# Moving part of a feed-forward stage from beside a convolution to beside a projection, with longer pieces of delta in memory

## The chip, the cores and the metric

The kernel runs on one core of a Trainium2 chip. A core has five engines that each work through an instruction queue of their own, in a fixed order: PE (TensorE, matrix products), DVE (VectorE), ACT (ScalarE), POOL (GpSimd) and SP (SyncE, which here issues every DMA). Sixteen DMA engines move data between HBM, the large memory, and SBUF, the memory on the chip. PE writes its products to PSUM, eight banks of 128 x 512 floats. The metric is the time of one execution in microseconds (us) on the device.

## The reference

The input is eight images of 96 channels and 64 x 64 positions. Layer 0 is a state-space block in four directions, layer 1 a linear attention and a feed-forward net on fp8:

```python
x = x + L0(group_norm(x))
  # L0, per image:
  xi, z = split(layernorm(x) @ in_proj_w.T + in_proj_b)          # 192 + 192 channels
  xi    = silu(depthwise_conv3x3(xi) + conv_b)
  xs    = [rows, columns, rows reversed, columns reversed]        # 4 directions, L = 4096 positions
  dts, B, C = split(x_proj_w[k] @ xs[k])                          # 6 + 16 + 16
  delta = softplus(dt_proj_w[k] @ dts + dt_proj_b[k])             # 192 channels
  h[t]  = exp(delta[t] * A) * h[t-1] + (delta[t] * u[t]) * B[t]   # 16 states a channel
  y[t]  = sum over states (h[t] * C[t]) + D * u[t]
  out   = out_proj(layernorm(sum over directions y) * silu(z))
t = tokens(x)
t = t + attention(layernorm(t))        # without softmax: q (k^T v)
t = t + ffn(layernorm(t))              # x, W1, W2 rounded to fp8 (5,2), sums to fp16, relu
```

## The kernel before

The eight images are worked on in four pairs; two images fill 384 rows, 192 channels each, in three tiles T of 128 partitions (the third holds 64 rows of each image). The positions are cut into eight chunks of F = 512. The loop from L883 runs five times, and in each pass lays the end of the pair before (`old`) beside the beginning of the next (`new`):

1. `back` of the old pair (L682: sums of the four directions, output projection, keys and values) together with `project` of the new one (L238: group norm, layer norm, input projection), L916.
2. `tail` of the old pair (L819) together with `convolve` of the new one (L311), L932.
3. `gates` (L349): 24 Silu activations on the convolution's result.
4. `prepare` (L365): for two orders of positions, eight chunks and two directions each, 32 steps in all. A step makes B, C and dts with three products (`pt`), copies them to `S`, makes delta with one product for each T (`pq`) and a Softplus, multiplies it by u (`du`), cuts delta into three bf16 parts (`dp`, on ACT, DVE and POOL by turns) and writes all of it to scratch in HBM (`bs`, `cs`, `du`, `dl`).
5. `scan` (L435): 128 steps (four directions, 32 chunks of TC = 128 positions), the recurrence itself, eight scan instructions a step on DVE, their factors made by PE and ACT (L570, L577), the driving term by POOL (L552).

The first pass has no old pair and the last no new one, so the last pass is `back` and `tail` alone.

`tail` works on 16 pieces (two images, eight chunks), each in three stages: attention's product `pa` and the sum `t`, and the layer norm (L668: product `ncp`, square, product `nvp`, Ln and Exp, product with `ncp` to the fp8 tile `tq`); the first fp8 product `pf` with relu; the second one and the sum `ot`, which is stored. A step of `tail` starts one piece and carries the two before it one stage further, so that 18 steps do the whole. `convolve` yields 19 times: two of the three tiles are summed on DVE, nine taps in two halves (L342, L344), the third on PE as nine products with diagonal matrices (L328). `together` (L870) alternates between two such generators, `m` steps of the second spread over `n` of the first, and then runs both to their ends.

The order in which the code emits is a priority. Outside `scan` a planner puts the instructions of each engine in order before the run, by that priority and by when it reckons their inputs and buffers to be there; on the chip each engine keeps that order. Three things bind it. Activations that need a table (Ln and Exp, Silu, Softplus) keep the order of the program among each other (`table`, L177; the tables of Ln and Exp are loaded at L180, the others by the activation's own line). Pools limit what is in flight: `tps` gives `tail` six PSUM banks, `p1cp` gives `convolve` two; `prepare` has three for `pt` and four for `pq`; SBUF tiles of both have two or three buffers. And all DMAs stand in one queue, on SP. `scan` orders by hand: in step s, `load(s + 1)` brings the next chunk's delta (`dm`, two buffers), `fetch` the driving term (`dut`), `load_bc` and `diagonal` B and C.

`dl`, delta in scratch, has the shape [4 directions, 32 chunks, 3 parts, 16, 24 rows, 128 positions] in bf16, so one row of one chunk is 256 bytes in a piece. The weights `winT`, `xw` and `dtw` are loaded and laid out once, ahead of the loop, and stay in SBUF.

## Time and profile before

| | us |
|---|---|
| median of 3 runs | 11845.06 |
| lowest, highest | 11842.54, 11851.63 |
| the profiled execution, its span | 11820.4, 11818.4 |
| first pair: scans begin | 639 |
| second pair: scans of the first end; convolution and tail from; gates from; first Softplus; last writes of delta; scans begin | 2535; 2980; 3162; 3183; 3508; 3534 |
| last pass: tail alone from | 11633 |

Over the whole span PE is busy 73%, DVE 74%, ACT 58%, POOL 68%, and the DMA queue's packets take 75.4% of the sixteen engines' time. A profile covers one execution. Its page has the busy time of each engine in 40 slices; a table by stage gives the same for chosen stretches, with the clock that the throttle granted to PE (1.00 is full speed). In rows of groups and of time, an entry like `L344 DVE SCALAR_TENSOR_TENSOR xi<-y,c_convw,xi` names the line, the engine, the operation and its output and inputs; what stands in brackets is how long the engine was idle before, and what it waited for. In rows of waits come the line that waited, what it waited for, the sum in us, how often and the longest.

### The profile page before, as it was taken

The numbers are of one execution on the slowest core, as the hardware profiler recorded it, in microseconds if no ns is written. First come the engines' busy times: TensorE is split into PE (matmuls) and PEld (weight loads), VectorE is DVE, ScalarE is ACT, GpSimd is POOL, SyncE is SP. The second block draws the span as 40 slices with busy tenths as digits, with TensorE's granted clock in tenths as the row PEclk, the third lists the DMA queues.
The fourth block names the chain that finished last, engine by engine and source line by source line (L and its number), as shares of the span: only waits on it lengthen the run. The fifth ranks groups of instructions, "written<-read, shape, count | busy, mean of one in ns | idle before, by whom it ended". The sixth has DMA issues, their size and how long they took to land. (4 is left out here: it accounts for less than half of the span.)

```text
span 11818.4 us, 387513 instructions
## 1 busy us (share of the span) xinstructions
PE 8675.0 (73%) x170112; PEld 5662.7 (48%) x170112; DVE 8756.4 (74%) x6465; ACT 6900.1 (58%) x12176; POOL 7986.7 (68%) x2770
## 2 busy tenths in 40 slices
PE   7856666779877666667986666667898666667787
PEld 2245555544225555554422555555442355555542
DVE  5489999963549999995355999999454699999922
ACT  3556666644456666664455666666445566666623
POOL 0489999960249999994025999999313699999910
PEclk8678888879768888888976888888896788888896
DMA  2988888875398888886459888888646988888862
GB/s 79 215 198 201 198 203 201 198 160 134 97 215 195 203 201 200 204 195 149 120 125 209 197 202 199 197 199 199 148 99 156 203 199 199 200 198 200 193 132 63
DMA packets 1655919, 2092.92 MB, mean 177 GB/s; under 512 B 962179, under 2 KB 1307348, under 8 KB 1651412
## 3 DMA queue, kind: packets, MB, share of 16 engines
q1 hardware_dynamic: 1654228, 2068.13, 75.4%
q8 instruction: 1335, 21.87, 0.9%
q14 instruction: 356, 2.92, 0.1%
HBM read 1604.17 MB, written 463.54 MB: 175 GB/s over the span
## 5 line engine op out<-in xcount | busy, mean ns | idle before, releaser
L588 DVE TENSOR_TENSOR_SCAN h<-da,dbu 128x774 f32<-128x774 f32 x4096 | 7028.4, 1760 | 646.5 <-ACT da L577 443.1
L552 POOL TENSOR_TENSOR dbu<-dut,bc 128x1536 f32<-128x1536 f32 x2048 | 7083.1, 3506 | 578.1 <-ACT dbu L549 478.7
L577 ACT ACTIVATE da<-da 128x768 f32<-128x768 f32 x4092 | 3254.2, 797 | 2155.9 <-PE da L570 2117.6
L606 PE MATMUL yp<-h,cw 128*32 128x48 f32 x131072 | 3145.2, 246 | 1126.0 <-issue 1110.7
L570 PE MATMUL da<-dm,aw 128*128 128x128 bf16 x24576 | 2502.0, 251 | 1447.2 <-DVE h L588 1098.1
L606 PEld LDWEIGHTS yp<-h,cw 128*32 128x32 f32 x131072 | 2548.9, 155 | 1673.2 <-issue 1408.7
L570 PEld LDWEIGHTS <-aw 128*128 128x128 bf16 x24576 | 1844.5, 111 | 1774.5 <-issue 1452.5
L506 ACT ACTIVATE cw<-bc,blk 128x512 f32<-128x512 f32 x2048 | 1472.8, 720 | 297.9 <-DMA bc<-cs 216.2
L745 POOL TENSOR_TENSOR yk<-yk 128x768 f32<-128x768 f32 x64 | 115.8, 1809 | 1268.2 <-DMA yk<-ys 1010.6
L427 POOL TENSOR_TENSOR dp<-rest,dp 128x512 bf16<-128x512 f32 x384 | 458.1, 1194 | 707.3 <-ACT dp L426 691.6
L425 DVE TENSOR_TENSOR rest<-delta,dp 128x512 f32<-128x512 f32 x384 | 301.1, 785 | 628.2 <-ACT dp L424 628.2
L404 PE MATMUL pq<-S,dtw 12*128 12x512 f32 x768 | 594.8, 882 | 140.2 <-ACT delta L408 75.3
L614 ACT ACTIVATE yev<-yp 128x384 f32<-128x384 f32 x1024 | 503.4, 492 | 243.1 <-PE yp L606 240.6
L858 POOL TENSOR_TENSOR ot<-t,y 96x512 f32<-96x512 f32 x64 | 128.1, 2002 | 612.0 <-DVE y L856 593.7
L786 DVE SCALAR_TENSOR_TENSOR g<-yc,c_onw,yrs 96x512 f32<-96x512 f32 x128 | 89.9, 742 | 483.2 <-ACT yrs L190 483.2
L404 PEld LDWEIGHTS pq<-S,dtw 12*128 12x128 f32 x768 | 162.4, 250 | 566.0 <-ACT delta L408 179.1
L426 ACT ACTIVATE dp<-rest 128x512 bf16<-128x512 f32 x384 | 241.6, 630 | 327.3 <-DVE rest L425 327.3
L672 ACT ACTIVATE nsq<-ncp 96x512 f32<-96x512 f32 x128 | 75.8, 592 | 572.8 <-PE ncp L670 559.6
L549 ACT COPY dbu<-h 128x12 f32<-128x12 f32 x1984 | 407.1, 205 | 0.0
L758 PEld LDWEIGHTS py<-ident,yk 128*24 128x24 f32 x8192 | 231.6, 108 | 241.7 <-issue 182.6
L758 PE MATMUL py<-ident,yk 128*24 128x128 f32 x8192 | 319.1, 290 | 31.5 <-DVE yk L744 25.7
L384 POOL COPY u<-xi 128x512 f32<-128x512 f32 x96 | 109.3, 1156 | 327.6 <-ACT xi L354 296.6
(136 smaller groups left out, 6684.3 us busy)
## 6 DMA issues: line engine op xcount, KB each, us to landing
dut<-du SPq DMA_DIRECT2D x1024, 768.0 KB
dm<-dl SPq DMA_DIRECT2D x512, 576.0 KB
dl<-dp SPq DMA_DIRECT2D x256, 384.0 KB
dm<-dl SPq DMA_DIRECT2D x512, 192.0 KB
ys<-yev SPq DMA_DIRECT2D x1024, 96.0 KB
du<-du SPq DMA_DIRECT2D x256, 256.0 KB
bc<-bs SPq DMA_DIRECT2D x512, 128.0 KB
bc<-cs SPq DMA_DIRECT2D x512, 128.0 KB
```

Source lines behind the costliest of these rows:

```text
L404: nc.tensor.matmul(pq, dtw[64:76, k, T], S[64:76], start=True, stop=True)
L425: nc.vector.tensor_tensor(rest, d, dp[:, :, 0], ALU.subtract)
L427: nc.gpsimd.tensor_tensor(dp[:, :, 2], rest, dp[:, :, 1], ALU.subtract)
L506: nc.scalar.activation(cw[i % 2][:, :, :, m, :].rearrange("p z j t -> p (z j) t"), bc[i][:, 1].rearrange("p z (j t) -> p (z j) t", j=NB), ...
L549: nc.scalar.copy(start, segs(hs[s - 1][:, :, r])[:, :, :, 1 if back else TC])
L552: nc.gpsimd.tensor_tensor(segs(t)[:, :, :, 1:], dut[g // 2][:, NI * (r % 2) : NI * (r % 2) + NI, :].unsqueeze(1) .to_broadcast([128, 2, NI ...
L570: nc.tensor.matmul(e[:, i], aw[k, r][:, i, z, :], dm[s][:, NI * r + i, :], start=True, stop=True,)
L577: nc.scalar.activation(e, e, AF.Exp)
L588: nc.vector.tensor_tensor_scan(hs[s][:, w, r][:, d], da[p % 3][:, o : o + W6][:, d], dbu[4 * s + r][:, w][:, d], 0.0, ALU.mult, ALU.add,)
L606: nc.tensor.matmul(y[32 * q : 32 * q + 32, 2 * NE * i : 2 * NE * i + 2 * NE] .rearrange("p (j r i) -> p i j r", j=2, r=NR), w[:, z, :, t], ...
L614: nc.scalar.activation(yev[s][:, :, o : o + 8, :].rearrange("p j i e -> p i j e"), y[:, 0 : 16 * NE].rearrange("p (i j e) -> p i j e", j=2 ...
L758: nc.tensor.matmul(o, yk[:, k, 4 * g + e, NE * j : NE * j + NE], ident, start=False, stop=(k + j == 4),)
```

## The change

Three things are done.

The tail is divided. Seven of its 18 steps are emitted beside the 19 steps of `convolve`; then the convolution's pools are closed and `gates` is emitted; then the other eleven steps beside the first 24 of `prepare`'s 32, which has become a generator and yields after each direction of a chunk. `tail` has four PSUM banks where there is a new pair and eight in the last pass; `prepare` has two for `pt`, and two for `pq` where a tail runs beside it (else four).

`dl` is cut into 16 pieces of WC = 256 positions instead of 32 of 128, so a row of a piece is 512 bytes, and `dp` is laid out and written accordingly. `scan` loads the delta of two chunks into one tile of 256 positions, in two halves: in step s it loads, for the pair of chunks that step s + 2 belongs to, the first twelve rows per partition if s is even and the last twelve if it is odd. Two such loads are issued ahead of the first step instead of one.

To have room for the larger `dm`, three weights leave the constant pool. `winT` is loaded in `project`. `xw` is laid out once, written to scratch (`xwd`) and read back at each `prepare`; `dtw` is read there from the input, by one DMA.

```diff
+WC = 256
-    winT = load("winT", [DIM, 2 * DI])
...
-    xw = const.tile([128, KD, 3, 76], F32, name="xw")
-    dtw = const.tile([128, KD, 3, 128], F32, name="dtw")
+    xwd = dram.tile([128, KD, 3, 76], F32, name="xwd", bufs=1)
...
+        nc.sync.dma_start(xwd, xw)
...
-    def prepare(xi, us, dl, du, bs, cs_):
+    def prepare(beside, xi, us, dl, du, bs, cs_):
...
-            ps = st.enter_context(tc.tile_pool(name="p2ps", bufs=3, space=PSUM))
-            pd = st.enter_context(tc.tile_pool(name="p2pd", bufs=4, space=PSUM))
+            ps = st.enter_context(tc.tile_pool(name="p2ps", bufs=2, space=PSUM))
+            pd = st.enter_context(tc.tile_pool(name="p2pd", bufs=2 if beside else 4, space=PSUM))
+            xw = tmp.tile([128, KD, 3, 76], F32, name="xw", bufs=1)
+            nc.sync.dma_start(xw, xwd)
+            dtw = tmp.tile([128, KD, 3, 128], F32, name="dtw", bufs=1)
+            nc.sync.dma_start(dtw[64:76], a["dtw"].rearrange("k r t c -> r k t c"))
...
-                            dp = tmp.tile([128, F // TC, 3, TC], BF16, name="dp")
+                            dp = tmp.tile([128, F // WC, 3, WC], BF16, name="dp")
...
                             spread(
-                                lambda o, n: dlv[k, j, :, o : o + n]
+                                lambda o, n: dlv[k, c * F // WC : (c + 1) * F // WC, :, o : o + n]
...
+                        yield
...
-                dm[s] = wk.tile([128, NE, TC], BF16, name="dm")
-                v = dl[k, c].rearrange("a m e t -> (a m) (e t)")
-                to = dm[s].rearrange("p e t -> p (e t)")
-                nc.sync.dma_start(to[0:96], v.unsqueeze(1).to_broadcast([48, 2, NE * TC]))
+                if s % 2 == 0:
+                    dm[s // 2] = wk.tile([128, NE, WC], BF16, name="dm")
+                e = slice(NE // 2 * (s % 2), NE // 2 * (s % 2) + NE // 2)
+                v = dl[k, c // 2, :, :, e].rearrange("a m e t -> (a m) (e t)")
+                to = dm[s // 2][:, e].rearrange("p e t -> p (e t)")
+                nc.sync.dma_start(to[0:96], v.unsqueeze(1).to_broadcast([48, 2, NE // 2 * WC]))
                 nc.sync.dma_start(to[96:128], v[0:32])
...
-                        e[:, i], aw[k, r][:, i, z, :], dm[s][:, NI * r + i, :],
+                        e[:, i], aw[k, r][:, i, z, :], dm[s // 2][:, NI * r + i, bass.ts(c % 2, TC)],
...
             load(0)
+            load(1)
...
-                            load(s + 1)
+                            load(s + 2)
...
-    def together(one, other, n, m):
+    def together(one, other, n, m, rest=True):
...
-        for g in (one, other):
+        for g in (one, other) if rest else (other,):
...
-                ("dl", [KD, NT, 3, 16, NE, TC], BF16), ("du", [KD, NT, 16, NE, TC], F32),
+                ("dl", [KD, NT * TC // WC, 3, 16, NE, WC], BF16), ("du", [KD, NT, 16, NE, TC], F32),
...
                     one = tail(
-                        pair - 1, old["t1"], old["tn"], pool("tt", 3), pool("tps", 6, space=PSUM)
+                        pair - 1, old["t1"], old["tn"],
+                        st.enter_context(tc.tile_pool(name="tt", bufs=3)),
+                        st.enter_context(tc.tile_pool(name="tps", bufs=4 if new else 8, space=PSUM)),
                     )
                 if new:
-                    other = convolve(
-                        xi, ybuf, pool("p1c", 1, side="right"), pool("p1cp", 2, space=PSUM)
-                    )
-                together(one, other, 18 if old else 1, 19)
-            pads.close()
-            if new:
-                gates(xi)
-                prepare(xi, new["us"], new["dl"], new["du"], new["bs"], new["cs"])
+
+                    with ExitStack() as sc:
+                        other = convolve(
+                            xi, ybuf, sc.enter_context(tc.tile_pool(name="p1c", bufs=1, side="right")),
+                            sc.enter_context(tc.tile_pool(name="p1cp", bufs=2, space=PSUM)),
+                        )
+                        together(one, other, 7, 19, rest=False)
+                    pads.close()
+                    gates(xi)
+                    other = prepare(
+                        bool(old), xi, new["us"], new["dl"], new["du"], new["bs"], new["cs"]
+                    )
+                together(one, other if new else none, 11 if old else 1, 24)
```

## The prediction

> **What bounds the kernel now.** I read the page first, then a table of busy times by stage, then inside the stages the chain that ended last, VectorE's and ScalarE's instructions in order of time, the waits and the DMA view. The page's slices show four long plateaus, the scans, and between them valleys of some 900 us in which VectorE is half idle and POOL nearly so; only what lies in the valleys is reshaped by the change.
>
> ```profile
> DVE  5489999963549999995355999999454699999922
> POOL 0489999960249999994025999999313699999910
> ```
>
> The table cuts the second valley into its stages (span, busy us and count of PE, PEld, DVE, ACT and POOL, then the granted clock, the DMA engines' share and GB/s):
>
> ```profile
> 2505.00:2980.00 475.00, 424.51 (x3810) 208.16 (x3808) 161.12 (x219) 204.88 (x325) 65.93 (x31) 0.92 0.56 127
> 2980.00:3100.00 120.00, 103.65 (x247) 39.93 (x245) 117.05 (x121) 44.62 (x77) 32.53 (x13) 0.92 0.20 58
> 3100.00:3163.00 63.00, 46.51 (x70) 13.26 (x70) 21.95 (x54) 23.49 (x40) 5.90 (x6) 0.54 0.12 35
> 3163.00:3182.00 19.00, 13.37 (x27) 4.34 (x26) 2.33 (x7) 18.81 (x33) 5.26 (x6) 0.82 0.21 76
> 3182.00:3508.00 326.00, 273.09 (x363) 71.45 (x361) 143.19 (x197) 188.93 (x319) 137.20 (x117) 0.64 0.99 222
> 11633.00:11819.00 186.00, 135.74 (x192) 37.62 (x192) 59.98 (x144) 64.90 (x112) 19.09 (x18) 0.50 0.17 51
> ```
>
> Row 1 is back with project, bound by PE and not touched. Row 2 is tail with convolve: DVE busy 117 of 120 us. Row 3 is the rest of the tail with nothing beside it: 63 us in which no engine is loaded. Row 4 is gates (ACT), row 5 prepare (DMA share 0.99), row 6 the last tail, alone. In VectorE's order of time the last convolution step starts at 3096.58, and the tail still runs at 3161.76:
>
> ```profile
> 3096.58 2.34 DVE L344 SCALAR_TENSOR_TENSOR xi<-y,c_convw,xi 128x2048 f32<-128x2048 f32 x1
> ...
> 3161.76 0.69 DVE L677 TENSOR_TENSOR tq<-ncp,nrs 96x512 fp8e5<-96x512 f32 x1 [5.20 <-ACT nrs L190]
> ```
>
> Why a lone tail is slow is read from the chain that ended last, whose steps repeat every 10.9 us, one feed-forward chunk after the other (11656.17 to 11667.04):
>
> ```profile
> 11656.17 1.44 PE pf L843 x3
> 11657.61 1.72 PE pa L834 x2
> 11660.19 2.00 PE ncp L670 x2
> 11662.86 2.04 PE nvp L674 x2
> 11667.04 1.44 PE pf L843 x3
> ```
>
> In prepare the DMA engines are full, and I need the price of a packet. Two stretches of 5 us with different mixes, 3213 to 3218 and 3243 to 3248 (packets under 512 B are dl's 256 B, the rest almost all du's 512 B):
>
> ```profile
> DMA packets 3607, 1.06 MB, mean 212 GB/s; under 512 B 3059, under 2 KB 3607, under 8 KB 3607
> q1 hardware_dynamic: 3607, 1.06, 102.7%
> ...
> DMA packets 2973, 1.09 MB, mean 218 GB/s; under 512 B 1829, under 2 KB 2973, under 8 KB 2973
> q1 hardware_dynamic: 2973, 1.09, 96.9%
> ```
>
> 3059a + 548b = 82,160 ns of engine time (16 x 5 us x 1.027) and 1829a + 1144b = 77,520 give a = 20.6 and b = 34.8 ns; a fit through 35 stretches of 7 us gives 20.7 and 33.0, which I use. The waits of 3200 to 3500 show what follows the DMA closely:
>
> ```profile
> ACT dp L426 <- DVE rest L425: 79.2, 92, 2.0
> ACT dp L424 <- DMA dl<-dp: 20.4, 45, 1.6
> ACT S L396 <- DMA cs<-S: 10.4, 1, 10.4
> ```
>
> ACT waits 31 us for DMAs, but 79 us for VectorE: faster packets free only the first.
>
> **The change, part by part.** The sum is made against the profiled execution, 11820.4 us (span 11818.4), which lies 24.7 us under the median 11845.06.
>
> A, eleven of 18 tail steps leave convolve (three valleys). VectorE begins convolve at 2980. What stays on it: 32 steps at 2.336 and four at 1.33, about 78 us with the usual 0.07 overlap; and seven tail steps of about 4 us (t 0.67, tq 0.68, three h at 0.35 to 0.5 and three hq at 0.42, y 0.34), less the unfinished two chunks, 26 us. End 3084. PE, 104 busy of 120 now, loses as much tail work and stays below. From the end of the tail (3162.3) to the first softplus (3182.6) it now takes 20.3 us of gates and tables, so the first softplus moves to 3104: 78 us each, 234 in all. Bounds: convolve ends no earlier than its 3099 now, 63 each; or the seven steps' rests are hidden as well, 84.
>
> B, dl in 512 B packets. One step of prepare (one of 32) writes 4608 packets of dl, 1536 of du, 128 of 1 KB (two 512 B prices): 154.5 us of engine time, 9.66 us on 16 engines; the trace has 9.45 from step to step (du of T=0 is issued at 3303.47, 3313.17, 3322.60, 3332.07). With 2304 packets at 33.0 it is 8.45. ACT without its 31 us of DMA waits comes to 8.5, so 8.5: minus 0.95 in each of 32 steps, 30 us in the first pair, where no tail runs beside. Bounds 0 (a dl packet costs twice as much when twice as long) and 39.
>
> C, the tail beside prepare, three pairs: 11 tail steps in 24 prepare steps, nine of them with a norm. DMA: 8.5 plus the tail's 288 packets of 2 KB per chunk at 108 ns (2016 of them in the 80 us from 3000), 1.9 us per tail step, gives 9.4 a step. ACT: prepare 5.85 busy a step (189 over 32), the tail 4.1 per chunk (64.9 over 16), and nine times two table loads of 1.28 us, since Ln and Exp must stand in program order between Softplus groups (rows at L180 and L305 show the same alternation in the first stage): 140 + 41 + 23 = 204 over 24 steps, 8.5. To this come waits that nothing may fill: 0.76 three times a step, 55 us, giving 10.8. PE's half clock, 1.06 us a pass in the last tail, leaves it near 10 too. I take 11.0, nearest to the ACT row with its waits unfilled. Behind a waiting Ln on ACT stand the copies to dp and the next Softplus; behind a waiting dp2 or ot on POOL, and the stores of them on SP, stand the writes of du and dl, which free their three buffers. SP's tail issues cost 0.3 us each, three a chunk, POOL's ot 1.15 to 3.1, both beside slack. Then 24 x 11.0 + 8 x 8.5 = 332 against 32 x 9.45 = 302: plus 30 each, 90. Bounds: 9.4 a step, minus 9 each; the tail's chain inserted whole, plus 113 each (below).
>
> The rule of the Trainium skill, "ScalarE: Activation LUTs", section "What ACT_TABLE_LOAD costs", speaks against this part: it counts a drain with each load, about 2.66 us a switch, and the rule below it says to finish one table set before changing. The rows show 1.283 and an activation that starts 1.30 after the load's start (3162.33, 3163.63). By the page the 18 loads would cost 48 instead of 23 us, some 75 us more over three pairs.
>
> D, PSUM. tps from 6 to 4 banks beside new work, pt from 3 to 2, pq from 4 to 2: pq for the next-but-one waits for a Softplus that comes every 2.8 us, a pair of passes takes 1.9, hidden; without cover, up to 1.9 a step, inside C's range. The last tail gets 8 banks instead of 6. A chunk uses seven; the next chunk's pa now starts only behind this one's pf, at 11657.61, though PE stood idle and the chunk's input was loaded. Six banks taken in turn would explain it: pa's would be that of ncp, held until tq is made. With eight it is free early. If pa and t go ahead, the 2.58 us from 11657.61 to 11660.19 leave each of 15 periods: 39 us. PE's busy time per chunk, 8.3, allows no more at this clock. I take 39; bounds 0 and 39.
>
> E, scan. The same bytes per step of dm, in the same 6 KB rows, one step earlier or more: 0, where PE waits for dm little (80 us in all, 8 times, at starts). At its start a second 768 KB stands ahead of dut on the queue, 3.6 us at 210 GB/s, four times: plus 14; bounds 0 and 14.
>
> F, weights. xw (467 KB) and dtw are loaded again in each pair, winT too; the first two land while gates keep ACT for 17 us. 0; without that cover 4 us a pair, 16.
>
> Sum: -234 - 30 + 90 - 39 + 14 = -199, 11621 on the profiled execution, 11646 against the median.
>
> **Rivals.**
> Slower: ACT stands through the tail's chain. Engines work in a fixed order, and if Ln stands in ACT's queue before its nvp is there, each tail step inserts its 10.92 us: 204 (24 x 8.5) + 120 + 23 = 347, 14.5 a step, 113 more a pair: -234 - 30 + 339 - 39 + 14 = +50, 11895. It decides from 13.8 a step. For it: ACT already waits 79 us for VectorE, in order. Against: pa to nvp hang on no table and can run ahead.
>
> The packets do not get cheaper, only longer: 41 ns for 512 B. Prepare alone stays at 9.45, beside the tail 11.6 (what DMA adds on top): plus 52 each, pair one 0: -234 + 156 - 39 + 14 = -103, 11742. Against: du's 512 B at 33.
>
> Everything fits: 9.4 a step; -234 - 30 - 27 - 39 + 14 = -316, 11529. For it: ACT's gaps are there to be filled, the first stage weaves two such chains.
>
> **How the numbers follow.** Forecast 0.45, slower rival 0.15, dear packets 0.15, everything fits 0.2; 0.05 for scans that change by themselves (their four lengths differ by some 20 us). About 0.2% (24 us) is what this kernel's measurement can tell from no change. Faster 0.80, same 0.05, slower 0.15. The likeliest alone has 11570 to 11720; the range must take in 11529 and 11742 with their own spread, 11500 to 11800.
>
> **What would show it.** First softplus some 104 us after convolve begins, and no lone tail rows; table loads up by about 54; in the first pair a step of prepare near 8.5 and under-512 packets down by 590,000; beside the tail 11 a step, with ACT busier than 0.75; the last tail's period near 8.3. I am wrong if ACT shows long waits for nvp or PE for ACT in prepare, if the DMA share stays at 0.99 in the first pair, or if the scans' steps lengthen.

## The result and the profile after

The changed kernel takes 11674.94 us (median of 4 runs, 11655.8 to 11685.34), the kernel before, on the same chip, 11843.8: a ratio of 0.986, with a 95% interval of 0.984 to 0.9881. That is 169 us less, and 29 more than the forecast of 11646. The profiled execution took 11665.74 us (span 11664.0), 154.7 less than the profiled execution before. The two traces, cut into stages, account for it:

| stage (us, before to after) | first pair | second | third | fourth | last pass |
|---|---|---|---|---|---|
| whole valley | 638.8 to 615.6 | 998.5 to 957.7 | 999.7 to 958.5 | 994.1 to 955.2 | 580.6 to 572.3 |
| VectorE's start on the convolution to first Softplus | | 202.5 to 120.4 | 203.0 to 121.5 | 202.6 to 120.4 | |
| first to last Softplus | 307.3 to 286.1 | 309.8 to 360.1 | 310.7 to 356.0 | 313.3 to 356.3 | |

The valleys lose 23.2, 40.8, 41.2, 38.9 and 8.3 us, 152.4 together; the four scans change by -4, +13, -10 and -1, which cancel. So all of it lies where the change was made: the convolution's stretch gives 82 us three times, and prepare takes 43 to 50 of them back.

The page's slices show the valleys as before, with VectorE and POOL half idle in them:

```profile
DVE  5489999963659889995366999999445699999922
POOL 0489999960259999994025999999303699999910
```

The table by stage of the second valley and the last pass (span; busy us and count of PE, PEld, DVE, ACT, POOL; granted clock, DMA share, GB/s):

```profile
2944.00:3046.00 102.00, 96.25 (x227) 39.01 (x227) 101.20 (x92) 35.16 (x60) 17.18 (x9) 0.94 0.17 50
3046.00:3064.00 18.00, 13.02 (x26) 3.96 (x26) 5.34 (x11) 17.95 (x30) 7.42 (x8) 0.77 0.55 208
3064.00:3303.00 239.00, 216.31 (x339) 62.55 (x338) 125.77 (x192) 160.25 (x268) 87.63 (x69) 0.68 0.74 191
3303.00:3435.00 132.00, 98.05 (x132) 24.44 (x131) 72.67 (x86) 74.30 (x129) 70.52 (x58) 0.66 0.85 216
11487.00:11664.00 177.00, 127.97 (x192) 35.83 (x190) 60.56 (x144) 64.90 (x112) 18.38 (x16) 0.55 0.17 49
```

The first row is the convolution with seven tail steps: VectorE is busy for 101 of 102 us, and the 63 us of a lone tail that followed are gone; gates (second row) follow at once. Rows three and four are prepare, with the tail and without. Neither ACT (160 of 239) nor the DMA engines (.74) are full beside the tail: prepare waits there. In VectorE's order of time the convolution's last operations now lie directly ahead of the tail's next step:

```profile
3041.86 4.60 DVE L346 SCALAR_TENSOR_TENSOR xi<-y,c_convw,xi 128x2048 f32<-128x2048 f32 x2
3046.38 0.34 DVE L866 TENSOR_SCALAR y<-y,b2q 96x512 f16<-96x512 f16 x1
```

Two stretches of 5 us of the first pair's prepare, 320 to 325 and 340 to 345, in the DMA view:

```profile
DMA packets 2425, 1.24 MB, mean 249 GB/s; under 512 B 125, under 2 KB 2425, under 8 KB 2425
q1 hardware_dynamic: 2425, 1.24, 97.5%
...
DMA packets 2514, 1.30 MB, mean 260 GB/s; under 512 B 102, under 2 KB 2514, under 8 KB 2514
q1 hardware_dynamic: 2514, 1.30, 95.9%
```

Almost every packet now has 512 B. Taking the few small ones at the 20.7 ns of before, the first gives (78,000 - 125 x 20.7) / 2300 = 32.8 ns, the second (76,720 - 102 x 20.7) / 2412 = 30.9. Over the whole run packets under 512 B fell from 962,179 to 372,484, by the 590,000 that were forecast.

The waits of the second valley's prepare beside the tail, 3064 to 3303:

```profile
POOL dp L433 <- ACT dp L432: 128.6, 45, 18.2
...
ACT delta L414 <- PE pq L410: 22.8, 14, 7.0
...
ACT y L865 <- PE pf L861: 14.3, 4, 10.3
ACT nsq L682 <- PE ncp L680: 13.9, 3, 9.3
```

Beside the tail ACT no longer waits for DMAs (31 us before); it waits for products of PE, twice for 9 to 10 us in one piece. One of the two, in the trace of all engines in order of time, is the costliest step of all (29.5 us from the Softplus at 3157.0 to the one at 3186.56):

```profile
3162.01 0.67 ACT L414 ACTIVATE delta<-pq,c_dtb 128x512 f32<-128x512 f32 x1
3162.70 1.28 ACT L180 ACT_TABLE_LOAD   x1
...
3174.58 0.98 SPq L842 DMA_DIRECT2D ta<-t  x1
...
3178.40 0.68 DVE L846 TENSOR_TENSOR t<-ta,pa 96x512 f32<-96x512 f32 x1 [7.70 <-DMA ta<-t]
...
3181.20 0.59 ACT L682 ACTIVATE nsq<-ncp 96x512 f32<-96x512 f32 x1 [9.35 <-PE ncp L680]
...
3183.90 0.68 ACT L189 ACTIVATE nrs<-nvp,eps 96x512 f32<-96x512 f32 x1 [2.11 <-PE nvp L684]
...
3185.27 1.28 ACT L414 ACT_TABLE_LOAD   x1
...
3186.56 1.27 ACT L414 ACTIVATE delta<-pq,c_dtb 128x512 f32<-128x512 f32 x2
```

The table of Ln is loaded at 3162.70, and from there no Softplus may run until the norm's Ln and Exp are through. But the norm's input isn't there: its `ta` stands in SP's queue behind the stores of prepare and is issued only at 3174.58. I call such a stretch, from the table of Ln to the next Softplus, a hold. The second valley's nine holds last 5.3, 5.8, 5.8, 5.8, 23.9, 10.0, 7.1, 5.8 and 5.8 us, 75.3 in all. ACT is idle for 19.2 us of that: 14.9 in the hold of 23.9, 2.9 in that of 10.0 and 1.1 in that of 7.1; in those of 5.3 and 5.8 it is busy throughout, with the norm, copies and activations that need no other table. The third's and fourth's come to 75.7 and 74.4, with 19.5 and 18.2 idle.

The chain that ended last in the lone tail, from one chunk to the next (11550.23 to 11561.09):

```profile
11550.23 1.44 PE pf L853 x3
11551.67 0.93 PE pa L844 x2
...
11554.21 2.03 PE ncp L680 x2
...
11556.91 2.04 PE nvp L684 x2
...
11561.09 0.39 PE pf L853
```

It is the chain of before, 10.86 us, `pa` behind `pf` as it was, though the banks are now eight.

### The profile page after: what moved, and what is told of

The parts are those of the page before. It is cut to its first block, busy times and chain, and to the rows that moved or that the text cites. A ratio compares the mean times of both kernels' runs of the same rounds, so it can differ in the third digit from the quotient of the medians.

```text
span 11664.0 us, 386998 instructions
## 1 busy us (share of the span) xinstructions
PE 8587.3 (74%) x170112; PEld 5661.1 (49%) x170112; DVE 8817.1 (76%) x6465; ACT 6931.4 (59%) x12227; POOL 7968.6 (68%) x2770
## 2 busy tenths in 40 slices
DMA packets 1362204, 2095.89 MB, mean 180 GB/s; under 512 B 372484, under 2 KB 1012997, under 8 KB 1357701
## 5 line engine op out<-in xcount | busy, mean ns | idle before, releaser
L561 POOL TENSOR_TENSOR dbu<-dut,bc 128x1536 f32<-128x1536 f32 x2048 | 7084.1, 3508 | 615.6 <-ACT dbu L558 460.9
L431 DVE TENSOR_TENSOR rest<-delta,dp 128x512 f32<-128x512 f32 x384 | 335.3, 876 | 420.4 <-ACT dp L430 420.2
L410 PE MATMUL pq<-S,dtw 12*128 12x512 f32 x768 | 559.0, 837 | 111.2 <-ACT delta L414 92.6
L868 POOL TENSOR_TENSOR ot<-t,y 96x512 f32<-96x512 f32 x64 | 101.8, 1590 | 483.7 <-DVE y L866 391.2
L682 ACT ACTIVATE nsq<-ncp 96x512 f32<-96x512 f32 x128 | 75.7, 592 | 523.6 <-PE ncp L680 496.8
```

The source lines that it names most:

```text
L410: nc.tensor.matmul(pq, dtw[64:76, k, T], S[64:76], start=True, stop=True)
L431: nc.vector.tensor_tensor(rest, d, dp[:, :, 0], ALU.subtract)
L561: nc.gpsimd.tensor_tensor(segs(t)[:, :, :, 1:], dut[g // 2][:, NI * (r % 2) : NI * (r % 2) + NI, :].unsqueeze(1) .to_broadcast([128, 2, NI ...
```

## The experiments

The totals below are medians with the ratio to the kernel before on the same chip. A stage tells more than a total here: in the run with six banks, whose instructions stand on every engine exactly as in the changed kernel, the four scans took 48 us longer together in the profiled execution. Stages have a spread too. That run and the one with four stages in the last pass alone keep the changed kernel's order in the second, third and fourth valley, and these three take 2871 us together in the changed kernel, 2891 and 2875 in the two; a prepare beside the tail takes 350.7 to 360.5. Less than 20 us in three valleys, or less than 10 in one prepare, can't be told from this spread.

### The two parts by themselves

Pieces alone: the tail stands whole beside the convolution again.

```diff
                     one = tail(
...
-                        st.enter_context(tc.tile_pool(name="tps", bufs=4 if new else 8, space=PSUM)),
+                        pair - 1, old["t1"], old["tn"], pool("tt", 3), pool("tps", 6, space=PSUM)
...
-                        together(one, other, 7, 19, rest=False)
...
-                together(one, other if new else none, 11 if old else 1, 24)
+                together(one, other, 18 if old else 1, 19)
+            pads.close()
+            if new:
+                gates(xi)
+                for _ in prepare(False, xi, new["us"], new["dl"], new["du"], new["bs"], new["cs"]):
+                    pass
```

> The change without its division of the tail: the tail of a pair stands beside the next convolve as before (its 18 and 19 steps in turn, six PSUM banks), prepare runs alone, delta is still written in pieces of 256 positions and loaded for two chunks, and the weights still come early. The pieces alone are then to be read. In the changed kernel the first pair's prepare, which has no tail beside it in either kernel, took 286.1 us from first to last softplus against 307.3 before (21.2 less). Theory 1 (the store's packets set the pace of a lone prepare): all four prepares lose about 21 us, 84 in all, and the median lies near 11,760, 11,745 to 11,775. Theory 2 (the gain of the first pair comes from what stands around it, such as the early weights, and not from the packets): the three later prepares stay at 310 and the median is near 11,820.

Measured: 11720.47 us, ratio 0.9904 (0.9881 to 0.9928). The prepares take 288.0, 288.5, 289.8 and 288.2 us, and the valleys 611.7, 973.7, 974.6, 976.4 and 579.9. The first theory holds in the stages: the lone prepares lose 19 to 25 us, and the DMA share falls from 0.99 to 0.91. The median lies 25 us under its range. The profiled execution is 97 us below that of before, and its valleys give 95 of it (27.1 + 24.8 + 25.1 + 17.7 + 0.7). The second valley's row of prepare:

```profile
3165.00:3454.00 289.00, 250.09 (x375) 68.48 (x373) 137.99 (x187) 180.60 (x315) 127.79 (x113) 0.71 0.91 238
```

Division alone: the tail is divided, `dl` stays in pieces of 128 and is loaded chunk by chunk.

```diff
-WC = 256
+WC = TC
...
-                if s % 2 == 0:
-                    dm[s // 2] = wk.tile([128, NE, WC], BF16, name="dm")
...
+                dm[s] = wk.tile([128, NE, TC], BF16, name="dm")
...
-            load(1)
...
-                            load(s + 2)
+                            load(s + 1)
```

> The change without its pieces: the tail divided between convolve (11 steps) and prepare (24 steps) with the changed kernel's PSUM banks, but delta written in pieces of 128 positions (packets of 256 bytes) and loaded chunk by chunk. Convolve must come out as in the changed kernel, 82 us sooner to the first softplus in three places, 246 in all. The prepares with a tail tell two theories apart. Theory 1 (beside the tail the compute engines and the order of their queues set the pace, and not the packets): from first to last softplus about as in the changed kernel, 356 to 360 us, so that only the first pair's 21 us are lost and the median is near 11,700, 11,685 to 11,715. Theory 2 (the packets set the pace there too): 21 us more in each, near 380, and the median is near 11,760, 11,745 to 11,780.

Measured: 11832.11 us, ratio 0.9999 (0.9983 to 1.0015). From the convolution's start to the first Softplus 121.3, 120.2 and 120.2 us, as in the changed kernel; but the prepares beside the tail take 401.8, 402.4 and 405.4. Neither theory had that much: 92 us more than before, where the changed kernel pays 46. So the division by itself is worth nothing, the pieces by themselves 115 us of the medians, and both together 169: each makes the other better. In the second valley the stretch with the tail and the one after it:

```profile
3085.00:3361.00 276.00, 224.35 (x352) 64.63 (x350) 127.06 (x197) 166.67 (x275) 89.56 (x73) 0.71 0.77 171
3361.00:3488.00 127.00, 93.11 (x119) 22.79 (x118) 55.78 (x71) 66.94 (x115) 64.93 (x50) 0.64 0.86 188
```

The DMA engines are not full beside the tail, .77, so the dear packets act in another way. VectorE's waits in the first of these stretches show it:

```profile
DVE t L843 <- DMA ta<-t: 19.6, 2, 9.9
```

There are two late loads of `ta` in place of one (7.7 us), and two long holds, 26.7 and 27.1 us. The nine holds of a valley take 103.5, 101.7 and 104.1 us, with ACT idle for 45.2, 43.3 and 45.8. Of the 45.7 us that prepare beside the tail costs more than in the changed kernel (means of three), 26 are this idle time; the other 20 are what a lone prepare pays for the dear packets too.

### PSUM banks

Six banks for the lone tail of the last pass:

```diff
-                        st.enter_context(tc.tile_pool(name="tps", bufs=4 if new else 8, space=PSUM)),
+                        st.enter_context(tc.tile_pool(name="tps", bufs=4 if new else 6, space=PSUM)),
```

> The changed kernel with six PSUM banks in place of eight for the lone tail of the last pair, and nothing else different. Theory of the prediction (the banks shorten a step of the lone tail, which was then to take 8.3 us in place of 10.95): the last valley becomes some 39 us longer. Theory from the trace (the steady step took 10.87 us with eight banks against 10.95 with six, as the order of the queues bounds it): 0 to 8 us more, a median within 8 us of the changed kernel's 11,675.

Measured: 11698.0 us, ratio 0.9884 (0.9858 to 0.991). The last valley takes 579.5 us in place of 572.3, a step 10.85 in place of 10.55 (mean of 15). The order on every engine is the same in both, and yet most of these 7 us are not the banks'. A period of the lone tail has two lengths: 10.86 us with eight banks and 10.92 with six where the granted clock is 0.50, 9.89 and 9.96 where it is 0.67. The changed kernel has five short periods of fifteen (one of them 10.17), this run one. At the same clock the banks are worth 0.06 us a period, 1 us in all; some 3.5 us are the clock, and 2.7 came before the first norm was through. The second theory holds for the valley; the median lies 23 us above the changed kernel's, as the scans were longer.

Two banks for `pq` in prepare, without a tail beside it (an edit of the run with the pieces alone):

```diff
-                for _ in prepare(False, xi, new["us"], new["dl"], new["du"], new["bs"], new["cs"]):
+                for _ in prepare(bool(old), xi, new["us"], new["dl"], new["du"], new["bs"], new["cs"]):
```

> The run with the pieces alone (tail whole beside convolve, prepare by itself), where the later three prepares get two PSUM banks for pq in place of four, as the changed kernel gives its prepare beside the tail; the first pair's keeps four. So the price of the fewer banks is read without the tail. With four banks these prepares took 288.5, 289.8 and 288.2 us from first to last softplus; with two and the tail beside them, in the changed kernel, 360, 356 and 356. Theory 1 (the banks are a good part of the 68 us that the tail costs there: ScalarE's wait of 22.8 us for pq and TensorE's of 28 for ScalarE in the changed kernel): 10 us or more longer in each, a median of 11,750 or above. Theory 2 (the banks are cheap, and the tail's own work costs the time): within 4 us of 289 each, a median of 11,710 to 11,730.

Measured: 11742.25 us, ratio 0.9916 (0.9897 to 0.9935). The three prepares take 289.2, 286.5 and 286.3 us, against 288.5, 289.8 and 288.2 with four banks: no longer. Prepare's rows in the second valley, with two banks here and with four above, have the same clock, .71, and the same DMA share, .91:

```profile
3172.00:3461.00 289.00, 257.94 (x374) 67.81 (x372) 136.17 (x187) 179.34 (x314) 126.43 (x113) 0.71 0.91 237
```

The median lies between the two forecasts (up to 11,730, and from 11,750), but its interval of the ratio overlaps that of the run with four banks, and the stages that the edit touches did not grow: the second theory. The banks beside the tail were tried as well, three for each in place of two and four, on top of the edits of the last section:

```diff
-            pd = st.enter_context(tc.tile_pool(name="p2pd", bufs=2 if beside else 4, space=PSUM))
+            pd = st.enter_context(tc.tile_pool(name="p2pd", bufs=3 if beside else 4, space=PSUM))
...
-                        st.enter_context(tc.tile_pool(name="tps", bufs=4 if new else 8, space=PSUM)),
+                        st.enter_context(tc.tile_pool(name="tps", bufs=3 if new else 8, space=PSUM)),
```

> The run that puts the two edits together, with the PSUM banks beside prepare shared out otherwise: three for pq and three for the tail, in place of two and four. Theory 1 (pq's two banks hold up prepare beside the tail: ScalarE waited 22.8 us for pq in the changed kernel's second valley): 8 us or more less in each of the three prepares than in the run beside it. Theory 2 (the tail's own banks, each held through squares, norm and output, are scarce in the same measure, or banks do not matter): within 5 us of it either way, or longer.

Measured: 11609.01 us, ratio 0.9813 (0.9787 to 0.9839), prepares of 353.1, 356.6 and 351.9 us against 347.0, 353.3 and 353.0 in the run beside it. No gain, so the second theory. It says little of the wait that the run was made for: in the run beside it, with two banks, ACT's wait for `pq` in the second valley had already fallen from 22.8 to 1.3 us.

### Table loads

Exp in the place of Softplus, the planner told that it needs the table of Ln:

```diff
-                            table("softplus", lambda: nc.scalar.activation(
-                                d, pq, AF.Softplus, bias=dtb[:, k, half(T) : half(T) + 1]
+                            table("ln", lambda: nc.scalar.activation(
+                                d, pq, AF.Exp, bias=dtb[:, k, half(T) : half(T) + 1]
```

> The changed kernel with Exp in the place of Softplus, which needs no other table than the norms' Ln and Exp, so that ScalarE loads no table between prepare and tail; the order marks of the two stay. It leaves out the softplus itself, so the values are not those of the reference. Theory 1 (the term of the prediction: the 17 further table loads of 1.28 us that a valley has gained stand on the path): at least 22 us less from first to last softplus in each of the three prepares beside the tail, the second valley's 360 becoming 338 or less, and a median of 11,610 or below. Theory 2 (ScalarE, busy for three quarters of that stretch, takes the loads in time in which it would wait for TensorE or VectorE anyway): under 8 us less in each, a median of 11,650 to 11,675. The first pair's prepare has no norms beside it and stays at 287 in both.

Measured: 11734.71 us, ratio 0.99 (0.9877 to 0.9924). The loads of a valley fall from 36 to 18, and yet the prepares take 378.2, 377.3 and 375.7 us, about 20 more than in the changed kernel. Neither theory expected it. The edit had moved more than the loads, since the planner made another order: in the second valley's prepare 63 of ACT's 397 activations, 48 of VectorE's 275 operations and 15 of SP's 336 DMAs stand out of the changed kernel's order. So it was repeated with the planner's grouping left as it was, only the function exchanged; the loads ahead of Softplus go and those of the norms stay:

```diff
-                                d, pq, AF.Softplus, bias=dtb[:, k, half(T) : half(T) + 1]
+                                d, pq, AF.Exp, bias=dtb[:, k, half(T) : half(T) + 1]
```

> The changed kernel with Exp for Softplus as in the earlier run, but with the planner still told that the two need different tables: the norms' loads stay (8 or 9 in a prepare beside the tail), prepare's own go, and the order of the instructions on every engine is nearly that of the changed kernel, which it was not in the earlier run. It leaves out the softplus itself. Nine loads of 1.28 us are 11.5 us of ScalarE's time in each of three prepares. Theory 1 (the table loads stand on the path): 10 to 14 us less in each prepare beside the tail, 346 to 350 in place of 356 to 360, a median about 35 below the changed kernel's. Theory 2 (they fall into ScalarE's waits): within 4 us of the changed kernel's. If these prepares become longer, as in the earlier run, the order of the queues sets them and not ScalarE's load.

Measured: 11753.11 us, ratio 0.9921 (0.989 to 0.9952). 27 loads a valley, and prepares of 370.5, 375.1 and 379.6 us: longer again, by 10 to 23. The order did not stay, as was expected: 54 of the 397 activations, 44 of the 275 operations and 14 of the 336 DMAs stand elsewhere, nearly as many as before. The first long hold is still there, though no table has to be loaded at its end now. ACT in order of time:

```profile
3179.86 1.28 ACT L180 ACT_TABLE_LOAD   x1
...
3198.38 0.59 ACT L682 ACTIVATE nsq<-ncp 96x512 f32<-96x512 f32 x1 [9.36 <-PE ncp L680]
...
3202.34 1.24 ACT L414 ACTIVATE delta<-pq,c_dtb 128x512 f32<-128x512 f32 x2
```

22.5 us without an activation for delta, and a second such hold of 23.6 us has come at 3289.71. VectorE's waits of that prepare have two late loads, as in the division alone:

```profile
DVE t L846 <- DMA ta<-t: 15.9, 2, 8.2
```

The short holds fell from 5.8 to 4.4 us as the load behind them was saved, and the second long one took that back: the holds sum to 80.1, 80.9 and 80.5 us, with 32.7, 33.7 and 33.2 idle. So a long hold needs no load at its end: it lasts until the norm's late input has come and its chain is through. What the loads themselves cost stays open: how prepare would run if only they went and no instruction moved was not measured.

### Earlier loads

The tail's two loads one step ahead in SP's order:

```diff
+            def fetch(b, c):
+                to = tns[(2 * c + b) % 4]
+                nc.sync.dma_start(to[0:DIM], tn[b, :, bass.ts(c, F)])
+                ta = tmp.tile([DIM, F], F32, name="ta")
+                nc.sync.dma_start(ta, t1[b, :, bass.ts(c, F)])
+                got[b, c] = to, ta
...
+                for j in range(0 if i == 0 else i + 1, min(i + 2, len(work))):
+                    fetch(*work[j])
                 if i < len(work):
                     going.append(ffn(*work[i]))
```

> The changed kernel with the two loads of a tail step (tn and t1) issued one step earlier in SyncE's order, nothing else. In the changed kernel's second valley one load of ta was issued only after SyncE had waited its way through stores of prepare; VectorE waited 7.7 us for it, and ScalarE, with the norm's table loaded, 9.35. Theory 1 (late loads are what the tail beside prepare pays): 10 to 25 us less in each of the three prepares beside the tail, a median of 11,600 to 11,645. Theory 2 (the loads are late once and the norm's chain and the split queues are paid on top): under 8 us less in each, a median of 11,650 to 11,675.

Measured: 11684.89 us, ratio 0.9863 (0.9839 to 0.9886). The prepares take 353.4, 343.4 and 353.1 us, 6.7, 12.6 and 3.2 less than in the changed kernel, and the three valleys 950.8, 943.8 and 948.8, 28 less together; the total doesn't show it, as the scans of this profiled execution took 44 us longer. VectorE never waits for `ta` here, and the hold of 23.9 us becomes 10.3. But the holds of the second valley become 5.3, 5.9, 5.9, 5.9, 10.3, 12.4, 5.9, 8.3 and 13.3, 73.2 in all with 16.3 idle, 3 less than in the changed kernel: the time moved to later norms. The three valleys, 2843 us, lie 28 to 47 below the three runs of the changed kernel's order, which is more than these differ; what else in the new order gave it stays open. Between the two theories, nearer the second: the late load is one cause of a long hold and the first to show, and when it goes the norm's input is late for other reasons.

### POOL's copies in the second half of prepare

```diff
-                            ut = tmp.tile([128, F], F32, name=f"u{T}", bufs=2)
-                            nc.gpsimd.tensor_copy(
-                                ut.rearrange("p (w h) -> p w h", h=HH),
-                                xi[T].rearrange("p (h w) -> p w h", w=HH)[:, bass.ts(c, ROWS), :],
-                            )
-                            u.append(ut)
+                            u.append(xi[T][:, cs])
```

> The changed kernel without POOL's copies of u into column order in the second half of prepare; that half then reads the row-order slices in their place, so the transposition of positions is left out and the values are not those of the reference. In the changed kernel a step of the first pair's prepare takes 8.2 us in the first half and 10.25 in the second, where the DMA share falls from .97 to .80 and VectorE's sum after a copy of POOL takes 1.17 to 1.66 us in place of 0.69. Theory 1 (POOL's copies and their hold on VectorE set the pace of the second half, no longer the packets): the second half's steps fall to about 8.2 us and the first pair's prepare from 287 to about 255, a valley of 582. Theory 2 (the packets set the pace in both halves): under 6 us less. Beside the tail either theory lets it lose less than in the first pair.

Measured: 11630.02 us, ratio 0.9814 (0.9791 to 0.9837). The first pair's prepare takes 265.8 us in place of 286.1, those beside the tail 338.0, 339.9 and 340.5. The table of busy times for the two halves of the first pair's prepare, of the changed kernel:

```profile
287.00:421.00 134.00, 126.19 (x211) 37.27 (x210) 61.72 (x93) 89.82 (x158) 52.92 (x46) 0.77 0.97 252
421.00:573.00 152.00, 123.72 (x164) 31.57 (x162) 75.44 (x94) 88.99 (x157) 72.77 (x66) 0.65 0.84 217
```

And of this run:

```profile
284.00:420.00 136.00, 132.28 (x209) 38.90 (x207) 61.80 (x93) 90.22 (x158) 52.51 (x45) 0.73 0.96 249
420.00:550.00 130.00, 112.49 (x167) 32.07 (x166) 63.00 (x95) 90.28 (x157) 54.97 (x48) 0.68 0.98 255
```

Without the copies the second half's step falls from 9.78 to 8.21 us and the DMA engines are full there again (.98 against .84). The first theory holds in kind; its 32 us came of a step of 10.25, where the mean over the half was 9.78. In VectorE's groups the sum that follows ACT's copy shows an effect of POOL. Of the changed kernel, from 425 to 565:

```profile
L431 DVE TENSOR_TENSOR rest<-delta,dp 128x512 f32<-128x512 f32 x43 | 44.3, 1030 | 71.3 <-ACT dp L430 71.3
```

Of this run, from 425 to 545 (busy us, mean ns of one, idle ahead):

```profile
L426 DVE TENSOR_TENSOR rest<-delta,dp 128x512 f32<-128x512 f32 x44 | 30.5, 692 | 59.8 <-ACT dp L425 59.8
```

1.03 us on average with POOL's copies, 0.69 without them. The mean hides three lengths. In that stretch 25 of the 43 sums take 0.69 us, those that share 0.6 us with a copy on POOL 1.17, and those that share 1.1 us with POOL's `dp` 1.66. Of the last kind, from VectorE's and POOL's orders of time:

```profile
479.50 1.66 DVE L431 TENSOR_TENSOR rest<-delta,dp 128x512 f32<-128x512 f32 x1 [1.19 <-ACT dp L430]
...
479.46 1.15 POOL L433 TENSOR_TENSOR dp<-rest,dp 128x512 bf16<-128x512 f32 x1
```

The copies put `dp` there, as they stand ahead of it on POOL. They also make it late: SP, which stores `dp`, waits 36.9 us for it from 450 to 560 in the changed kernel and 2.2 from 430 to 540 in this run. Which of the two sets the pace of the second half, the longer sums or the late `dp`, no run separates.

### The tail in four stages

In the last pass alone, `pa` and `t` of a chunk are emitted one step ahead of its norm:

```diff
+                t2 = tmp.tile([DIM, F], F32, name="t2", bufs=4 if ahead else 3)
                 nc.vector.tensor_tensor(t2, ta, pa[:DIM], ALU.add)
+                if ahead:
+                    yield
...
-            for i in range(len(work) + 2):
+            for i in range(len(work) + 2 + ahead):
...
+                        ahead=not new,
```

> The changed kernel with the lone tail of the last pair cut into four stages in place of three: the matmul into pa and the sum t are issued one step ahead of the norm that reads them; the tails beside prepare are as they were. Theory 1 (in the lone tail a step takes 10.87 us as pa stands behind pf in TensorE's order, and t, squares and norm then follow in series): the steady step falls to between 8.3 and 9.5 us, 22 to 40 us less in the last valley, and a median of 11,635 to 11,653. Theory 2 (a single engine is full, or the loads of the tail come late): the step stays at 10.9 and the median at 11,675 or, with one more step to fill, up to 8 us above it.

Measured: 11622.85 us, ratio 0.9819 (0.9796 to 0.9843). The last valley takes 516.4 us in place of 572.3: 56 less, where 22 to 40 were expected. The first theory holds and was too small. The table's row of the lone tail:

```profile
11537.00:11632.00 95.00, 71.50 (x178) 25.19 (x177) 58.81 (x134) 59.45 (x105) 16.09 (x14) 0.90 0.26 76
```

The chain that ended last, over one chunk of 5.91 us:

```profile
11571.73 1.10 PE nvp L684 x2
11572.83 0.86 PE pa L844 x2
11573.69 0.66 PE pf L863 x3
...
11577.64 1.10 PE nvp L684 x2
```

The same two passes into `nvp` took 2.04 us above and take 1.10 here: the granted clock is 0.90 where it was 0.55. So two things came together. The rows of the first period, the only one wholly at the slow clock, and of the next seven:

```profile
11536.00:11545.00 9.00, 7.61 (x12) 2.47 (x12) 3.33 (x10) 3.48 (x6) 0.00 (x0) 0.50 0.15 44
11545.00:11586.00 41.00, 30.11 (x86) 10.90 (x85) 27.66 (x63) 27.65 (x49) 8.05 (x7) 1.00 0.35 101
```

The first takes 8.94 us, against 10.86 with the old order at that clock; the next ones take 5.9. By this one period the order, which takes `pa`, `t` and the waits around them out of the series, is worth up to 1.9 us by itself, 29 in fifteen periods and within the forecast. (Up to, as the stages are still filling then: PE is busy for 7.6 us, where a slow period of the old order has 8.5.) The rest, about as much, is the clock, which was not forecast.

In every pair:

```diff
-                        ahead=not new,
+                        ahead=True,
...
-                together(one, other if new else none, 11 if old else 1, 24)
+                together(one, other if new else none, 12 if old else 1, 26)
```

> The changed kernel with the four-stage tail (the matmul into pa and the sum t one step ahead of the norm) in every pair, beside convolve and beside prepare as well; the tail has then 19 steps, 7 beside convolve and 12 over 26 steps of prepare. With it the lone tail's steady step took 6.4 us in place of 10.6 and the last valley 516 in place of 572. Theory 1 (the tail's chain in series is also what holds up convolve and prepare beside it, as the engines work in order): 10 us or more less in each convolve and 20 or more in each prepare, 90 or more below the run with the lone tail alone, a median of 11,530 or below. Theory 2 (beside other work the chain is covered, and the tail costs its engines' time and table loads): the three valleys stay within 10 us of 957 and the median is near 11,623.

Measured: 11609.27 us, ratio 0.9801 (0.9776 to 0.9825). The three valleys take 955.9, 956.7 and 956.1 us, as before this edit (957.3, 954.4 and 963.6): the convolution's stretch loses some 6, the prepares take 364.6, 359.0 and 362.4. The second theory holds. The chain that ruled the lone tail isn't what holds up prepare, and a step that starts earlier doesn't shorten the holds (ten in the second valley, 87.5 us).

### The best version

Four stages in the last pass, and the loads a step earlier everywhere, both diffs as above.

> The two edits that took time away put together: the four-stage tail in the last pair alone, and the tail's two loads issued a step earlier everywhere. By the single runs: the last valley 508 to 516 us in place of 572 (56 to 64 less), and the three valleys before it 951, 944 and 949 in place of 957.7, 958.5 and 955.2 (28 less). If the two add, the median lies 84 to 92 below the changed kernel's, 11,583 to 11,591, some 2.2% below the kernel before. If the early loads' gain was chance of the order, near 11,615.

Measured: 11603.58 us, ratio 0.9796 (0.9774 to 0.9818), 2.0% below the kernel before, where the change as given is 1.4% below. The last valley takes 513.5 us, the three before it 946.8, 952.7 and 954.8. Of the 28 us that the loads had gained, 17 are left beside the changed kernel's valleys. By the totals it can't be told from the four stages alone (0.9819); by the three valleys it is ahead by 21 us, where runs of one order differ by 19.

## Why the prediction was right

The sum of the prediction was -199 us, the profiled executions differ by 154.7. By its own steps:

**A, convolution: -234 forecast, -246 measured.** VectorE was the bound, 101 busy of 102 us. The stretch from 2943.9 to 3046.5 is 102.6 us against the forecast's 104, and 17.8 us of gates and tables against 20.3 follow: 82 us each, within the bounds. (The 104 us to the first Softplus in the prediction's last part was a slip: the 104 is the convolution's end, and its own 3104 less 2980 gives 124. Measured 120.4.)

**B, packets: -30 forecast, -21 measured.** The price of a 512 B packet, 33.0, came out at 30.9 to 32.8 ns. The step fell by 1.13 us in the first half (9.49 to 8.36, forecast 9.45 to 8.5), but only from 9.91 to 9.78 in the second, where the DMA engines had stood at .97 and POOL's copies were next behind them. The mis-sized term is "minus 0.95 in each of 32 steps": it holds in 16. The run without the copies shows what was late next. Beside the tail the pieces save more, as the division alone shows: 46 us, of which 26 are ACT's idle time in holds, a second long one above all.

**C, the tail beside prepare: +90 forecast, +139 measured** (50.3, 45.3 and 43.0). A step beside the tail takes 11.7 us in place of 11.0 (24 x 0.7, 17 us), and the last ones 10.15 in place of 8.5 (7 x 1.65, 11.5 us), which is B's error again; the steps of before, 9.8 in these pairs and not 9.45, give 11 back. The term that was mis-sized is "waits that nothing may fill", 55 us. ACT's first 24 steps in the second valley, from Softplus to Softplus:

| us | in all | work | idle in holds | other idle |
|---|---|---|---|---|
| prediction | 264 | 204 | | 60 |
| changed kernel | 283 | 186 | 19 | 78 |
| pieces alone, no tail beside | 214.5 | 137 | | 78 |
| division alone | 319 | 188 | 44 | 87 |
| kernel before, no tail beside | 235 | 140 | | 95 |
| Softplus exchanged for Exp, second run | 293 | 176 | 32 | 85 |

The changed kernel's row less that of the pieces alone is the price of the tail: 49 us of work on ACT, 20.5 of it in sixteen table loads, 19 us of idle time in holds, and next to nothing else. The tail's work filled none of the 78 us in which ACT stands idle in a lone prepare; the third and fourth valleys show the same to within 5 us (74 and 76 against 79 and 78). With the dear packets, the division alone against the kernel before, it filled 8 of 95. The prediction had ACT's work 18 us too high and the waits 37 too low. The second run with Exp doesn't follow the rule, so it describes these orders and is no law.

The loads are there, 17 more in a valley, 51 against the forecast 54. The prediction named the Softplus behind a waiting Ln, but did not price that a norm between two Softplus groups keeps the next Softplus back until its whole chain is done: 5.8 us, all of them filled with other work, if its input is there, and 23.9, with 14.9 idle, if not. That the wait for the input does this, and not the load, is read from the hold's rows above; the second run with Exp has it without a load at its end.

Against this part the prediction set the Trainium skill, "ScalarE: Activation LUTs", section "What ACT_TABLE_LOAD costs", by which a switch takes 2.66 us with its drain. The rows show a load of 1.283 us and an activation that starts 1.29 after the load's start (3062.98 and 3064.27), with no drain. So C's miss is not the drain.

**D, the last tail: -39 forecast, -8.3 measured.** The failed step is "Six banks taken in turn would explain it". `pa` still stands behind `pf` with eight banks, and at the same clock they take 0.06 us from a period, 1 us in all. Of the 8.3 us measured some 4.5 are periods at a clock of 0.67 in place of 0.50, and 3 came before the first norm was through. PE works its queue in order, and the program emits a chunk's `pa` after the older chunks' `pf`. The rest of the step was nearly right: once the order lets `pa` and `t` go ahead of the norm, a period at the slow clock takes 8.94 us, where the prediction had 8.3 as the least "at this clock". What it did not see is that the clock would change with the order.

**E, scan's start: +14 forecast, 0 measured.** From the last `dp` to the first scan 32.5 us in both traces of the first pair; the second 768 KB ahead of `dut` is hidden. The scans changed by -2 together, as forecast. **F, weights: 0**, as forecast.

**The rivals.** "The packets do not get cheaper" is refuted by their price and by the pieces alone. (Its 11.6 us a step was mispriced as well: it adds a whole tail step's 1.9 us to each step of prepare, where C spreads eleven over 24, 0.9 each.) "Everything fits" needed 9.4 us a step; it was 11.7. The slower rival, ACT standing through the tail's chain, had a mechanism that does cost, 19 us of ACT's idle time a valley: it was counter-argued with "pa to nvp hang on no table and can run ahead", and that is true of seven norms in nine. One stands 23.9 us and one 10. Its price was too high since it applied the stand to every step. One of the prediction's own signs of being wrong did come: beside the tail ACT waited 13.9 us for `ncp` and 4.5 for `nvp`, and was busy for 0.67 of the time, not for more than 0.75.

So the sum missed the profiled execution by 44 us. A was right and large; C's cost was 49 too low, D's gain 31 and B's 9 too high, against A's 12 and E's 14 the other way and 11 that the stretches of back and project gave, which the sum did not hold; 8 more lie in small rests. A's mechanism was right, B's held in half of the steps, C's had the work and mis-sized the waits, D's was wrong. That the total came so near is luck in part, since 89 us of misses one way met 45 the other.

## What to carry to other kernels

Where a stream is laid into another that shares an engine with it in a fixed order, do not count on the engine's idle time to take it up: here the added work, table loads and all, came on top whole. To it comes the idle time of the stretches between a change of table and the change back; look there at what the stretch's inputs stand behind in the DMA queue. Moving work under other work gains only if the price there is lower: a tail step cost 82 / 11 = 7.5 us where it stood, beside the convolution and alone after it, 6.2 beside prepare with 512 B packets (68 more than the 289 of a lone prepare, over 11) and 8.4 with 256 B ones (92 / 11), so that one part of this change made the other pay. And before more buffers are given to a loop, look in the chain for whether it waits for a buffer or stands in the order of emission: here eight banks gained 1 us and one `yield` 56, about half of it by the clock that rose with it.

## What was not expected of the hardware

**The granted clock of PE rose by more than a half with a change of order.** In the lone tail it was 0.50 in the kernel before, 0.55 in the changed one, 0.52 and 0.51 in two runs with three stages, and 0.90 and 0.92 in two with four. PE's share of busy time was the same at both clocks (121.8 of 163 us against 71.5 of 95), and from the first `tq` on PE's longest idle stretch is 0.93 us in the kernel before, 1.63 in the changed one and 0.85 in the first run with four stages. A pair of passes into `nvp` takes 2.04 or 1.10 us accordingly. The busy share does not tell the two clocks apart, and gaps of 0.93 and 0.85 us hardly do: what decides the grant is open.

The Trainium skill, "TensorE: Matmul & The Clock Gate", section "Why this matters for your kernels", advises against idle gaps of more than about 3 us between bursts of products, if the clock is not to drop. Here it stayed at 0.50 with gaps of 0.93 us at most, and in the run with four stages it fell from 1.00 to 0.71 over a period without a gap above 0.85; the measurement decides.

**Work on POOL lengthened VectorE's sum beside it,** from 0.69 us to 1.17 where 0.6 us of a copy fell beside it, and to 1.66 where 1.1 us of a sum did. Without the copies the first pair's prepare is 20 us shorter, though POOL itself was far from full (72.8 of 152 us in the second half); the longer sums are 14.5 us of VectorE's time there.

**An edit that takes work from an engine can lengthen a stage.** The two runs with Exp took 20 and 9 us of ACT's work out of a prepare beside the tail and made it 18 to 21 and 10 to 23 us longer. The order of the instructions had changed with the edit; that this is the reason is argued, not shown.
